# A softmax turned through DRAM: whole rows out and four strided loads back, against four strided stores and whole rows back

## The chip, the cores and the metric

The kernel runs on one core of one Trainium2 chip, in fp32. The metric is the device time of one execution in microseconds, taken as the median of several runs. A profiled execution is a run of its own; its span (first to last instruction of the program) is a little shorter than its device time.

## The reference, cut to what matters

The input is x of 8 batches, 256 positions, 256 features. Four residual blocks follow one another, each on a layer norm of x: attention A (16 heads of 128), a gated FFN that keeps the 32 largest of 512 logits, attention B (16 heads of 16, block causal mask, rotary embedding), and the same FFN again.

```
x = x + attn_a(layernorm(x))      # softmax(q k^T / sqrt(128)) v, then Wout
x = x + ffn(layernorm(x))         # top 32 of 512 logits, softmax, genes, tanh gate
x = x + attn_b(layernorm(x))      # masked softmax(q k^T / 4) v, then w_o
x = x + ffn(layernorm(x))
```

In both attentions TensorE needs the softmax with keys on the partitions, to multiply it with v; it is made with queries on the partitions. It has to be turned: each 256 x 256 matrix of A, each 128 x 128 piece of B. This turn is what the change is about.

## The kernel before

**Tiles and loops.** The program goes over the 8 batches; in each, 256 positions are two tiles of 128 partitions. `attn_a` (L492) makes per head q and k (`qk_proj`, matmuls L522, copied by ACT at L530), scores (`soft`, L543), the softmax (`softmax`: maximum L739 on DVE, exponential L745 on ACT, reciprocal L751 on DVE, the product L756 on GpSimd), per pair of heads the turn and the product with v (`attend` L551, matmuls L568, copied by ACT at L577), and per four heads the output projection (`project`, L589). `ffn` (L773) is a serial chain, mostly on DVE: L810 (MAX8) and L827 (match and replace) alternate four times; its matmuls are L784, L799, L841, L855, L869. `attn_b` (L905) works on four groups of 32 rows at a time: scores L1015, softmax (L1126, L1132, L1138, L1143), the turn of two groups at a time, and the product with v in `attend` (L1067, matmuls L1077).

**The turn.** `turn` (L442) takes two softmax tiles of 128 x 512. DVE's 32 x 32 block transpose (L450) turns each within its blocks and writes it to T [128, 2, 512], the blocks laid so that a row of T holds four chunks c, one for each group of 32 partitions that it must go to. What remains is to swap partition group g with chunk c. This goes through a DRAM tile D of 512 KB: one store of T (L454), and, when it has landed, four loads (L460), one for each c, into 32 partitions of PT, each picking 256 runs of 512 B. PT is then the moving operand of L568 or L1077. Each of the seven batches 0 to 6 has 8 such turns in A and 6 in B, 98 in all. The last batch turns on TensorE instead (L680, L1040) and has none.

**Buffers.** T has two buffers, PT six, D six. DVE may write T again once the store has landed; a load into PT waits for the matmuls that read the buffer last.

**What sets the order.** The order of every engine is worked out ahead by `Plan` (L53 to L206). Each operation is given to `do` with a cost: how long it holds its engine and how long until its result is there. `order` (L106) is a greedy list: the operation that can start first goes first, of those within 1 ns the one of the best priority. It follows buffers as well as data. For transfers, the queue SP is held for the first number; the second is time on one common data path (bytes / 330 GB/s, so 1.59 us for 512 KB and 0.40 for 128 KB), and the landing is 2.0 us after that (`FLIGHT`, L161 to L163). In the turn, each store and load has 450 ns for SP. The planned order is then kept: all loads and stores are issued by SP's one queue, in that order, and an instruction that waits there holds all behind it. Where TensorE has a planned gap of 0.8 us or more, `keep_warm` (L184) puts in transposes of the identity (profile line L1169).

The other transfers on that queue are the loads of x (L286, one of 128 KB for each tile, 128 runs of 1 KB) and the stores of the output (L1151, the same size).

Of the kernel before, what the change touches and what calls it, by code (L numbers as in the profile page):

```python
# [17 lines left out]
P = 128  # L18
TT = S // P
# [6 lines left out]
SQ = 32  # L26
# [183 lines left out]
def kernel(  # L210
# [19 lines left out]

    const = ctx.enter_context(tc.tile_pool(name="const", bufs=1))
    work = ctx.enter_context(tc.tile_pool(name="work", bufs=1))
    psum = ctx.enter_context(tc.tile_pool(name="psum", bufs=1, space=bass.MemoryType.PSUM))
    dram = ctx.enter_context(tc.tile_pool(name="dram", bufs=1, space=bass.MemoryType.DRAM))

    def sb(shape, tag, bufs):
        return plan.buf(work, shape, tag, bufs)
# [201 lines left out]
            pe, reads, [key],  # L439
        )  # L440

    def turn(sources, pT, views, pri, keys):  # L442

        T = sb([P, 2, 512], "T", 2)
        D = plan.buf(dram, [P, 2, 512], "D", 6)
        for j, (p, view) in enumerate(zip(sources, views)):
            do(
                "DVE", dve(512), lambda j=j, view=view: [nc.vector.transpose(*view(T()[:, j]))],  # L450
                pri, [(p, 0)], [(T, j)],
            )
        do(
            "SP", (450.0, 524288 / plan.RATE), lambda: [nc.sync.dma_start(D(), T())],  # L454
            pri, [(T, 0), (T, 1)], [(D, 0)],
        )
        for c in range(P // SQ):
            do(
                "SP", (450.0, 131072 / plan.RATE),
                lambda c=c: [nc.sync.dma_start(  # L460
                    pT()[ts(c, SQ)].rearrange("p h (g f) -> p h g f", f=P),
                    D().rearrange("(g i) h (c f) -> c i h g f", i=SQ, f=P)[c])],
                pri, [(D, 0)], [keys[c]],
            )


    def normed_a(b):
# [24 lines left out]
    def attn_a(b):  # L492
        xT, pe, ew = normed_a(b)
        vs, qks, ps_, ao = {}, {}, {}, {}

        def v_proj(g):
            for t in range(TT):
                v = sb([P, HG * DA], "Av", 4)
                pv = bank("A")
                for c in range(DC):  # L500
                    do(
                        "PE", mm(512),
                        lambda c=c, t=t, pv=pv: [nc.tensor.matmul(  # L503
                            pv(), xT()[:, c, ts(t, P)], wA[2, g][:, c, :],
                            start=c == 0, stop=c == DC - 1)],
                        pe(g * HG, 0.5), [(xT, 0), ("wA", 2, g)], [(pv, 0)], [v],
                    )
                do(
                    "ACT", act(512), lambda v=v, pv=pv: [nc.scalar.copy(v(), pv())],
                    ew(g * HG, 0.5), [(pv, 0)], [(v, 0)],  # L510
                )
                vs[g, t] = v

        def qk_proj(h):
            g, i = divmod(h, HG)
            pq = bank("A")
            qk = sb([P, 2, S], "Aqk", 4)
            for kind in range(2):
                for c in range(DC):
                    do(  # L520
                        "PE", mm(256),
                        lambda kind=kind, c=c: [nc.tensor.matmul(  # L522
                            pq()[:, ts(kind, S)], wA[kind, g][:, c, ts(i, DA)], xT()[:, c, :],
                            start=c == 0, stop=c == DC - 1)],
                        pe(h, 0), [(xT, 0), ("wA", kind, g)], [(pq, kind)], [qk],
                    )

            do(
                "ACT", act(512),
                lambda: [nc.scalar.activation(  # L530
                    qk().rearrange("p k s -> p (k s)"), pq(), AF.Copy, scale=float(DA ** -0.25))],
                ew(h, 0), [(pq, 0), (pq, 1)], [(qk, 0)],
            )
            qks[h] = qk

        def soft(h):
            qk = qks[h]
            sc = bank("A")
            p = scores_of("A")
            for t in range(TT):  # L540
                do(
                    "PE", mm(256),
                    lambda t=t: [nc.tensor.matmul(  # L543
                        sc()[:, ts(t, S)], qk()[:, 0, ts(t, P)], qk()[:, 1, :],
                        start=True, stop=True)],
                    pe(h, 1), [(qk, 0)], [(sc, t)], [p],
                )
            softmax(sc, [(sc, 0), (sc, 1)], p, TT, S, "A", ew(h, 1))
            ps_[h] = p

        def attend(h0):  # L551
            po = bank("A")
            a = sb([P, 2, S], "Aao", 3)
            pT = sb([P, 2, 512], "PT", 6)
            turn(
                [ps_[h0], ps_[h0 + 1]], pT,
                [lambda T, p=ps_[h0 + j]: (
                    T.rearrange("p (c k t q) -> p t k c q", c=4, k=TT, t=TT),
                    p().rearrange("p t (k c q) -> p t k c q", k=TT, c=4)) for j in range(2)],
                ew(h0 + 1, 2), [(pT, c) for c in range(4)],  # L560
            )
            for j in range(2):
                h = h0 + j
                g, i = h // HG, h % HG
                for k in range(TT):
                    do(
                        "PE", mm(256),
                        lambda j=j, k=k, g=g, i=i: [nc.tensor.matmul(  # L568
                            po()[:, ts(j, S)].rearrange("p (t g q) -> p t g q", t=TT, g=4),
                            vs[g, k]()[:, ts(i, DA)],  # L570
                            pT()[:, j].rearrange("p (g k t q) -> p k t g q", g=4, k=TT, t=TT)[:, k],
                            start=k == 0, stop=k == TT - 1)],
                        pe(h, 3), [*((pT, c) for c in range(4)), (vs[g, k], 0)], [(po, j)], [a],
                    )
            do(
                "ACT", act(512),
                lambda: [nc.scalar.copy(a().rearrange("p j q -> p (j q)"), po())],  # L577
                ew(h0 + 1, 3), [(po, 0), (po, 1)], [(a, 0)],
            )
            ao[h0] = a  # L580

        def project(g):
            hs = range(g * HG, (g + 1) * HG)
            py = bank("A")
            for t in range(TT):
                for h in hs:
                    do(
                        "PE", mm(256),
                        lambda t=t, h=h: [nc.tensor.matmul(  # L589
                            py()[:, ts(t, DIM)], ao[h - h % 2]()[:, h % 2, ts(t, P)],  # L590
                            woutT[:, h, :], start=h == hs[0], stop=h == hs[-1])],
                        pe(hs[-1], 4), [(ao[h - h % 2], 0), ("wout", g)], [(py, t)],
                    )
            for t in range(TT):
                x = xs[b, t]
                do(
                    "DVE", dve(256),
                    lambda t=t, x=x: [nc.vector.tensor_tensor(
                        x(), x(), py()[:, ts(t, DIM)], ALU.add)],
                    ew(hs[-1], 4), [(py, 0), (py, 1)], [(x, 0)],  # L600
                )

        for h in range(HA):
            if h % HG == 0:
                v_proj(h // HG)
            qk_proj(h)
            soft(h)
            if h % 2:
                attend(h - 1)
            if h % HG == HG - 1:  # L610
                project(h // HG)
# [293 lines left out]
    def attn_b(b, t):  # L905
# [94 lines left out]
        def scores(c, pT):  # L1000
# [50 lines left out]
            if b < B - 1:  # L1051
                for g in range(0, NR, 2):
                    turn(
                        ps_[g : g + 2], pT[g // 2],
                        [lambda T, p=p: (
                            T.rearrange("p (c i q) -> p i c q", c=4, i=4),
                            p().rearrange("p a (i c q) -> p (a i) c q", i=TT, c=4))
                         for p in ps_[g : g + 2]],
                        ew, [(pT[g // 2], ("c", c)) for c in range(4)],
                    )  # L1060

        def turned_p(pT, g, i):
            if b == B - 1:
                return pT[g // 2]()[:, g % 2, ts(i, P)]
            return pT[g // 2]()[:, g % 2].rearrange("p (g i q) -> p i g q", g=4, i=4)[:, i]

        def attend(c, pT):  # L1067

# [2 lines left out]
            def emit():  # L1071
                n = t + 1
                for par in range(2):
# [9 lines left out]

            do(
                "PE", (450.0 * (t + 1) + 150, 450.0 * (t + 1) + 150 + plan.DRAIN), emit, pe(5),
                [*((pair, k) for pair in pT for k in (0, 1, *(("c", c) for c in range(4)))),
                 *((vbs[b, k], par) for k in range(t + 1) for par in range(2))],
                [(po, 0)], [ctxt],
            )
# [136 lines left out]
```

## Time and profile before

| | us |
|---|---|
| median of 3 runs | 1022.26 (1022.11 to 1028.04) |
| the profiled execution, device time | 1023.49 |
| its span | 1021.7 |
| matmuls of L1169 (identity), busy | 28.7, of it 26.8 after 894 us |
| POOL, ACT busy | 380.6, 468.8 |
| DMA queue of SP: 133936 packets, 117.71 MB | 36.3% of 16 engines' span |
| SP waiting for a store of T to land (L460) | 155.0, 67 times |
| SP waiting for a transpose on DVE (L454) | 199.0, 42 times |
| the chain that ended last: PE, DVE, DMA, SP's queue | 55%, 16%, 14%, 7% |

A row of a group or a line gives engine, operation, written tile <- read tiles, count, and durations. PE is TensorE's matmuls, DVE VectorE, ACT ScalarE, POOL GpSimd, SP the queue engine. "A <- B: 11.7, 11, 1.8" in the waits means that A's engine stood idle before A until B was done, 11.7 us in total, in 11 places, 1.8 us at the longest. A wait for several things is put down to the last. Engines are pipelined, so a busy matmul of 380 ns follows another one after 214 ns; only the last one of a run shows its full length.

### The profile page before, as it was taken

The numbers are of one execution on the slowest core, as the hardware profiler recorded it, in microseconds if no ns is written. First come the engines' busy times: TensorE is split into PE (matmuls) and PEld (weight loads), VectorE is DVE, ScalarE is ACT, GpSimd is POOL, SyncE is SP. The second block draws the span as 40 slices with busy tenths as digits, with TensorE's granted clock in tenths as the row PEclk, the third lists the DMA queues.
The fourth block names the chain that finished last, engine by engine and source line by source line (L and its number), as shares of the span: only waits on it lengthen the run. The fifth ranks groups of instructions, "written<-read, shape, count | busy, mean of one in ns | idle before, by whom it ended". The sixth has DMA issues, their size and how long they took to land.

```text
span 1021.7 us, 16959 instructions
## 1 busy us (share of the span) xinstructions
PE 971.1 (95%) x5843; PEld 730.8 (72%) x5843; DVE 681.7 (67%) x1670; ACT 468.8 (46%) x1503; POOL 380.6 (37%) x484
## 2 busy tenths in 40 slices
PE   7999999999999999999999999999999999999786
PEld 6777677676777777676776777667777668786664
DVE  2523867657676876759666686865867686688755
ACT  3433455443654445534644445634455335542261
POOL 2502245231553345323643335423354225542150
PEclk9999999999999999999999999999999999999988
DMA  9723225622266224642266223633136400420000
GB/s 331 253 95 104 83 81 183 191 78 68 93 216 187 78 68 145 189 131 93 83 185 187 82 84 129 203 113 119 56 134 201 126 6 21 136 93 11 1 2 11
DMA packets 134021, 118.78 MB, mean 116 GB/s; under 512 B 10160, under 2 KB 117808, under 8 KB 133936
## 3 DMA queue, kind: packets, MB, share of 16 engines
q1 hardware_dynamic: 133936, 117.71, 36.3%
q8 instruction: 46, 0.75, 0.3%
q14 instruction: 39, 0.32, 0.1%
HBM read 64.20 MB, written 53.48 MB: 115 GB/s over the span
## 4 chain that ended last, share of the span: by engine, by line
PE 55%; DVE 16%; DMA 14%; SPq 7%; issue 3%; POOL 3%; ACT 2%; POOLq 0%; DVEq 0%; ACTq 0%
PE ps L522 10%; PE ps L568 6%; DMA D<-T 6%; DMA PT<-D 6%; PE ps L589 6%; SPq L460 5%; PE ps L543 5%; PE ps L503 5%; DVE Fleft L827 4%; DVE Fm L810 4%; PE ps L799 3%; PE ps L869 2%; PE ps L1077 2%; PE ps L937 2%; PE ps L643 2%
## 5 line engine op out<-in xcount | busy, mean ns | idle before, releaser
L756 POOL TENSOR_TENSOR p<-p,Asm 128x512 f32<-128x512 f32 x128 | 135.0, 1056 | 303.3 <-DVE Asm L751 298.8
L522 PE MATMUL ps<-AxT,wqk 128*128 128x256 f32 x896 | 220.9, 381 | 0.0
L522 PEld LDWEIGHTS ps<-AxT,wqk 128*128 128x128 f32 x896 | 168.2, 191 | 26.2 <-issue 4.7
L450 DVE STREAM_TRANSPOSE T<-p 128x512 f32<-128x512 f32 x196 | 136.0, 702 | 57.3 <-POOL p L756 38.1
L745 ACT ACTIVATE p<-ps,Anm 128x256 f32<-128x256 f32 x256 | 119.1, 474 | 83.9 <-DVE Anm L739 80.0
L1143 POOL TENSOR_TENSOR p<-p,Bsm 128x512 f32<-128x512 f32 x96 | 99.0, 1042 | 102.8 <-DVE Bsm L1138 102.5
L739 DVE TENSOR_REDUCE Anm<-ps 128x2 f32<-128x512 f32 x128 | 87.3, 683 | 61.7 <-PE ps L543 58.7
L568 PE MATMUL ps<-PT,Av 128*128 128x256 f32 x448 | 110.3, 385 | 15.4 <-DMA PT<-D 12.0
L1132 ACT ACTIVATE p<-ps,Bnm 128x128 f32<-128x128 f32 (+1 forms) x256 | 106.2, 438 | 39.9 <-DVE Bnm L1126 29.6
L543 PE MATMUL ps<-Aqk 128*128 128x256 f32 x448 | 120.4, 382 | 0.0
L568 PEld LDWEIGHTS ps<-PT,Av 128*128 128x128 f32 x448 | 81.9, 190 | 46.0 <-issue 25.4
L589 PE MATMUL ps<-woutT,Aao 128*128 128x256 f32 x448 | 112.9, 385 | 0.1
L530 ACT ACTIVATE Aqk<-ps 128x512 f32<-128x512 f32 x112 | 67.3, 601 | 97.7 <-PE ps L522 97.3
L503 PE MATMUL ps<-wv,AxT 128*128 128x512 f32 x224 | 106.5, 594 | 0.0
L543 PEld LDWEIGHTS ps<-Aqk 128*128 128x128 f32 x448 | 82.9, 190 | 24.8 <-issue 14.6
L589 PEld LDWEIGHTS ps<-woutT,Aao 128*128 128x128 f32 x448 | 82.1, 190 | 21.4 <-issue 7.7
L1126 DVE TENSOR_REDUCE Bnm<-ps 128x2 f32<-128x512 f32 (+1 forms) x96 | 66.3, 690 | 3.0
L810 DVE MAX8 Fm<-Fleft 128x8 f32<-128x512 f32 x96 | 66.2, 690 | 2.3
L577 ACT COPY Aao<-ps 128x512 f32<-128x512 f32 x56 | 32.9, 587 | 70.8 <-PE ps L568 70.8
L827 DVE MATCH_REPLACE8 Fleft<-Fm,Fleft 128x512 f32<-128x512 f32 x96 | 64.9, 676 | 0.0
L799 PE MATMUL ps<-wcT,FxT 128*128 128x512 f32 x128 | 61.5, 598 | 0.8 <-ACT FxT L790 0.8
L503 PEld LDWEIGHTS ps<-wv,AxT 128*128 128x128 f32 x224 | 41.5, 190 | 28.3 <-issue 25.0
(118 smaller groups left out, 1380.6 us busy)
## 6 DMA issues: line engine op xcount, KB each, us to landing
D<-T SPq DMA_DIRECT2D x98, 512.0 KB, 3.0
PT<-D SPq DMA_DIRECT2D x392, 128.0 KB, 3.2
wqk<-in_wqkvT_dram SPq DMA_DIRECT2D x8, 512.0 KB, 9.2
x<-in_x_dram SPq DMA_DIRECT2D x16, 128.0 KB, 2.3
wv<-in_wqkvT_dram SPq DMA_DIRECT2D x4, 512.0 KB, 9.7
woutT<-in_woutT_dram SPq DMA_DIRECT2D x4, 512.0 KB, 10.3
out_dram<-x SPq DMA_DIRECT2D x16, 128.0 KB, 1.7
wcT<-in_wcT_dram SPq DMA_DIRECT2D x1, 512.0 KB, 9.5
```

Source lines behind the costliest of these rows:

```text
L450: "DVE", dve(512), lambda j=j, view=view: [nc.vector.transpose(*view(T()[:, j]))],
L503: lambda c=c, t=t, pv=pv: [nc.tensor.matmul(pv(), xT()[:, c, ts(t, P)], wA[2, g][:, c, :], start=c == 0, stop=c == DC - 1)],
L522: lambda kind=kind, c=c: [nc.tensor.matmul(pq()[:, ts(kind, S)], wA[kind, g][:, c, ts(i, DA)], xT()[:, c, :], start=c == 0, stop=c == DC - ...
L543: lambda t=t: [nc.tensor.matmul(sc()[:, ts(t, S)], qk()[:, 0, ts(t, P)], qk()[:, 1, :], start=True, stop=True)],
L568: lambda j=j, k=k, g=g, i=i: [nc.tensor.matmul(po()[:, ts(j, S)].rearrange("p (t g q) -> p t g q", t=TT, g=4), vs[g, k]()[:, ts(i, DA)], p ...
L589: lambda t=t, h=h: [nc.tensor.matmul(py()[:, ts(t, DIM)], ao[h - h % 2]()[:, h % 2, ts(t, P)], woutT[:, h, :], start=h == hs[0], stop=h == ...
L745: lambda i=i: [nc.scalar.activation(p()[:, i, :], s3()[:, i, :], AF.Exp, bias=nm()[:, i : i + 1], accum_out=sm()[:, i : i + 1])],
L756: lambda: [nc.gpsimd.tensor_tensor(p(), p(), sm().unsqueeze(2).to_broadcast((P, n, k)), ALU.mult)],
L810: lambda r=r, src=src: [nc.vector.max(m8[r](), src())],
L827: lambda r=r, src=src: [nc.vector.match_replace(left(), m8[r](), src(), TAKEN)],
L1132: lambda i=i: [nc.scalar.activation(p3()[:, i, :], s3()[:, i, :], AF.Exp, bias=nm()[:, i : i + 1], accum_out=sm()[:, i : i + 1])],
L1143: lambda: [nc.gpsimd.tensor_tensor(p3(), p3(), sm().unsqueeze(2).to_broadcast((P, n, k)), ALU.mult)],
```

## The change

In `turn` the two sides of the round trip change places. T is laid out as [128, 4, 256]: chunk c is the outer step, and within it the two heads (or groups) lie beside each other, so that a run for one destination is 256 elements (1 KB) rather than two of 128. Four stores, one for each partition group g of 32, write the runs of T to D where they belong: row (c, i), column group g. One load of 128 rows of 4 KB then brings D back to PT as it is. D's layout becomes the final one of PT, (g, h, f), and the matmuls of both attentions read PT by it: their moving operand steps 256 instead of 128 elements from one partition group's piece to the next. The planner's numbers follow: 360 ns of SP for each of the five transfers in place of 450, the bytes moved to the other side (128 KB for a store, 512 KB for the load); the load depends on all four stores, each store on both transposes, and PT has two keys, both written by the one load, in place of four. The line that opens the DRAM pool moves up by one.

```diff
--- before.py
+++ after.py
@@ -230,8 +230,8 @@
 
     const = ctx.enter_context(tc.tile_pool(name="const", bufs=1))
     work = ctx.enter_context(tc.tile_pool(name="work", bufs=1))
+    dram = ctx.enter_context(tc.tile_pool(name="dram", bufs=1, space=bass.MemoryType.DRAM))
     psum = ctx.enter_context(tc.tile_pool(name="psum", bufs=1, space=bass.MemoryType.PSUM))
-    dram = ctx.enter_context(tc.tile_pool(name="dram", bufs=1, space=bass.MemoryType.DRAM))
 
     def sb(shape, tag, bufs):
         return plan.buf(work, shape, tag, bufs)
@@ -439,29 +439,32 @@
             pe, reads, [key],
         )
 
-    def turn(sources, pT, views, pri, keys):
-
-
-
-        T = sb([P, 2, 512], "T", 2)
-        D = plan.buf(dram, [P, 2, 512], "D", 6)
+    def turn(sources, pT, views, pri):
+
+
+
+        T = sb([P, 4, 256], "T", 2)
+        D = plan.buf(dram, [P, 4, 256], "D", 6)
         for j, (p, view) in enumerate(zip(sources, views)):
             do(
-                "DVE", dve(512), lambda j=j, view=view: [nc.vector.transpose(*view(T()[:, j]))],
+                "DVE", dve(512),
+                lambda j=j, view=view: [nc.vector.transpose(
+                    *view(T().rearrange("p c (h f) -> p h c f", h=2)[:, j]))],
                 pri, [(p, 0)], [(T, j)],
             )
-        do(
-            "SP", (450.0, 524288 / plan.RATE), lambda: [nc.sync.dma_start(D(), T())],
-            pri, [(T, 0), (T, 1)], [(D, 0)],
-        )
-        for c in range(P // SQ):
-            do(
-                "SP", (450.0, 131072 / plan.RATE),
-                lambda c=c: [nc.sync.dma_start(
-                    pT()[ts(c, SQ)].rearrange("p h (g f) -> p h g f", f=P),
-                    D().rearrange("(g i) h (c f) -> c i h g f", i=SQ, f=P)[c])],
-                pri, [(D, 0)], [keys[c]],
-            )
+        for g in range(4):
+            do(
+                "SP", (360.0, 131072 / plan.RATE),
+                lambda g=g: [nc.sync.dma_start(
+                    D().rearrange("(c i) g f -> g i c f", i=SQ)[g], T()[ts(g, SQ)])],
+                pri, [(T, 0), (T, 1)], [(D, g)],
+            )
+        do(
+            "SP", (360.0, 524288 / plan.RATE),
+            lambda: [nc.sync.dma_start(
+                pT().rearrange("p h f -> p (h f)"), D().rearrange("p g f -> p (g f)"))],
+            pri, [(D, g) for g in range(4)], [(pT, 0), (pT, 1)],
+        )
 
 
     def normed_a(b):
@@ -555,9 +558,9 @@
             turn(
                 [ps_[h0], ps_[h0 + 1]], pT,
                 [lambda T, p=ps_[h0 + j]: (
-                    T.rearrange("p (c k t q) -> p t k c q", c=4, k=TT, t=TT),
+                    T.rearrange("p c (k t q) -> p t k c q", k=TT, t=TT),
                     p().rearrange("p t (k c q) -> p t k c q", k=TT, c=4)) for j in range(2)],
-                ew(h0 + 1, 2), [(pT, c) for c in range(4)],
+                ew(h0 + 1, 2),
             )
             for j in range(2):
                 h = h0 + j
@@ -568,9 +571,10 @@
                         lambda j=j, k=k, g=g, i=i: [nc.tensor.matmul(
                             po()[:, ts(j, S)].rearrange("p (t g q) -> p t g q", t=TT, g=4),
                             vs[g, k]()[:, ts(i, DA)],
-                            pT()[:, j].rearrange("p (g k t q) -> p k t g q", g=4, k=TT, t=TT)[:, k],
+                            pT().rearrange("p h f -> p (h f)").rearrange(
+                                "p (g h k t q) -> p h k t g q", g=4, h=2, k=TT, t=TT)[:, j, k],
                             start=k == 0, stop=k == TT - 1)],
-                        pe(h, 3), [*((pT, c) for c in range(4)), (vs[g, k], 0)], [(po, j)], [a],
+                        pe(h, 3), [(pT, 0), (pT, 1), (vs[g, k], 0)], [(po, j)], [a],
                     )
             do(
                 "ACT", act(512),
@@ -1053,16 +1057,17 @@
                     turn(
                         ps_[g : g + 2], pT[g // 2],
                         [lambda T, p=p: (
-                            T.rearrange("p (c i q) -> p i c q", c=4, i=4),
+                            T.rearrange("p c (i q) -> p i c q", i=4),
                             p().rearrange("p a (i c q) -> p (a i) c q", i=TT, c=4))
                          for p in ps_[g : g + 2]],
-                        ew, [(pT[g // 2], ("c", c)) for c in range(4)],
+                        ew,
                     )
 
         def turned_p(pT, g, i):
             if b == B - 1:
                 return pT[g // 2]()[:, g % 2, ts(i, P)]
-            return pT[g // 2]()[:, g % 2].rearrange("p (g i q) -> p i g q", g=4, i=4)[:, i]
+            return pT[g // 2]().rearrange("p h f -> p (h f)").rearrange(
+                "p (g h i q) -> p h i g q", g=4, h=2, i=4)[:, g % 2, i]
 
         def attend(c, pT):
 
@@ -1083,7 +1088,7 @@
 
             do(
                 "PE", (450.0 * (t + 1) + 150, 450.0 * (t + 1) + 150 + plan.DRAIN), emit, pe(5),
-                [*((pair, k) for pair in pT for k in (0, 1, *(("c", c) for c in range(4)))),
+                [*((pair, k) for pair in pT for k in range(2)),
                  *((vbs[b, k], par) for k in range(t + 1) for par in range(2))],
                 [(po, 0)], [ctxt],
             )
```

## The prediction

> **What bounds the kernel now.** I first read the page's busy shares, then TensorE's waits in the stretch where turns run (51 to 894 us), then one turn on the chain of waits, then the transfers one by one.
>
> The first row of the page:
>
> ```profile
> PE 971.1 (95%) x5843; PEld 730.8 (72%) x5843; DVE 681.7 (67%) x1670; ACT 468.8 (46%) x1503; POOL 380.6 (37%) x484
> ```
>
> TensorE sets the pace; no other engine is near full. What can be won is TensorE's idle time: in 51 to 894 us the table of windows has PE busy 818.5 of 843.0 us, so 24.5 us idle. The waits of PE in that window (us in total, times, longest):
>
> ```profile
> PE ps L568 <- DMA PT<-D: 11.7, 11, 1.8
> PE ps L1077 <- DMA PT<-D: 6.2, 7, 1.6
> PE ps L855 <- ACT FwT L847: 2.3, 5, 0.6
> ```
>
> 17.9 of the 24.5 us end with the landing of a turned softmax, in 18 waits of 1.0 us on average, none over 1.8. Outside it, another 0.5 us waits for PT. So the turn bounds nothing in most places, but it is late by about a microsecond in every fifth of the 98 turns. The ends are different: 894 to 1021.7 us hold no turn for TensorE beyond the first few us, and there its idle time (20.6 us by the windows) belongs to DVE, ACT and POOL.
>
> One such turn on the chain of waits (start, us, what):
>
> ```profile
> 116.89 0.62 DVE T L450
> 117.51 0.02 issue
> 117.53 4.76 DMA D<-T
> ...
> 122.34 0.56 SPq L460
> 122.90 0.05 issue
> 122.95 0.61 SPq L460
> 123.56 0.05 issue
> 123.61 0.60 SPq L460
> 124.21 0.04 issue
> 124.26 3.09 DMA PT<-D
> 127.34 0.04 issue
> 127.39 1.99 PE ps L568 x8
> ```
>
> From the transpose's end to the first matmul 9.9 us go by in three pieces: the store's landing, SP issuing three more loads behind the first (1.92 us), and the last load's landing. Over all 98 turns, the last transpose's end to the last landing takes 9.65 us in the mean and 7.5 at least: 0.81 until SP gets to the store, 3.19 for the store, 0.36 until the first load is issued, 5.30 for the four loads.
>
> **The change, part by part.** What each transfer costs, from the rows of the two lines (count, min/median/max ns to issue; then us to landing), and the page's part 6:
>
> ```profile
> L454 SPq DMA_DIRECT2D D<-T x98: 319/326/1219, 35.4 to 905.9; - x98
> DMA to landing us min/median/max: 2.6/3.0/5.0
> ```
> ```profile
> L460 SPq DMA_DIRECT2D PT<-D x392: 557/607/1702, 39.5 to 910.5; - x196
> DMA to landing us min/median/max: 2.7/3.2/4.7
> ```
> ```profile
> x<-in_x_dram SPq DMA_DIRECT2D x16, 128.0 KB, 2.3
> out_dram<-x SPq DMA_DIRECT2D x16, 128.0 KB, 1.7
> ```
>
> (1) Issue. 128 runs of 4 KB cost SP 0.326 us, 256 runs of 512 B cost 0.607. A new store has 32 rows x 4 runs = 128 runs: at least 0.326, at most 0.607; I take 0.35, since x and the output, also 128 runs, take 0.34. With 0.03 between issues, four stores take 4 x 0.35 = 1.4 us and the load 0.33. Per turn 1.8 us of SP instead of 0.33 + 4 x 0.64 = 2.9; over 98 turns 176 instead of 284 us.
>
> (2) Data. In windows holding one kind of packet alone, busy share x 16 engines / packets gives 29 ns for 512 B (92.0 to 98.5 us), 47 ns for 1 KB (an output store, 204.7 to 206.5) and 160 ns for 4 KB (109.3 to 112.0). Per turn and engine: before 8 x 160 + 64 x 29 = 3.1 us, after 32 x 47 + 8 x 160 = 2.8. A small gain.
>
> (3) The store stage. An output store of the same size and run length lands in 1.7 us undisturbed. The fourth new store is issued at 3 x 0.35 = 1.05 and lands at 2.75 if alone; the engines need 4 x 0.38 = 1.5 us for all four, about the rate of the issue, so I take 2.9. Before: 2.6 undisturbed. This part of the change costs 0.3 us. The store's rows are read from 32 partitions and written 4 KB apart; no row of the trace stores so, the nearest being the four loads (32 partitions, 512 B runs), whose packets fit the same line through the sizes. Bounds: 2.6 and, if each packet took twice its time, 4.4.
>
> (4) The load stage. An x load lands in 1.97 us undisturbed, 8 packets of 1 KB per engine (0.4 us) within it. With 8 of 4 KB (1.3 us): 1.97 - 0.4 + 1.3 = 2.9 us. Bounds: 2.6 (what the equally large store takes) and 3.6. Before: 4.8 to 5.0 undisturbed, 1.9 of them SP's issue of the later three.
>
> Sum, undisturbed: before 2.6 + 0.05 + 5.0 = 7.7 us, after 2.9 + 0.06 + 2.9 = 5.9: 1.8 us less. In the mean, with the same disturbance on each piece (x 1.2 on stores, x 1.1 on the load) and a shorter wait for SP (0.5): 0.5 + 3.5 + 0.3 + 3.3 = 7.6 instead of 9.65: 2.0 us less.
>
> [...] Were the four stores to run wholly one behind another, the stage would be 4 x 1.7 = 6.8 us and the turn 9.8, worse than 7.7. The trace's own four partition slices do not behave so: issued 0.64 apart, each lands about 3.1 us after its issue, all four in 5.0 and not 4 x 2.7 = 10.8. They share engines but overlap their fixed part. I go by the row. [...] Here the same 128 KB take 1.7 us to DRAM and 2.0 from it, so I keep 2.9.
>
> (5) Waits. The load waits for four stores instead of one: three more semaphores, at 17 to 28 ns each by SP's rows, under 0.1 us. Behind it in SP's queue stand other turns' stores, x loads and output stores; "L460 <- DMA D<-T" holds SP for 155 us now. The hold behind the last issue shrinks from 2.3 to about 1.5 us per turn, so all of them gain. T (two buffers) is freed 0.3 us later; DVE waits for it six times, 10.4 us in all, so 2 us more on an engine with a third of its time free. TensorE waits on one semaphore in place of four per turn: nothing, PE's semaphore instructions (51 ns) run under earlier matmuls. The transposes and matmuls keep their numbers and sizes; only steps change from 128 to 256 elements, with runs of 32 as before: nothing, and were each of the 196 transposes 10% slower (0.07 us) DVE would still cover 14 us.
>
> (6) The plan's numbers. In the planner's own arithmetic a turn is 7.4 us before (1.59 + 2.0, then four loads 0.45 apart) and 7.25 after. So it leaves about the same work between a softmax and its use; but any change of a due time reorders the list, and the order of all engines comes out anew. Nothing in the trace prices that. I bound it by TensorE's idle time in this stretch that is no turn's, 24.5 - 17.9 = 6.6 us: it could be 6 us less or twice that, 13 us, more; I take 0.
>
> **Sum.** With the order unchanged, TensorE does the same work between a softmax and its use, so a wait shrinks by what the turn got faster. All 18 waits are at most 1.8 us and the turn gains 1.8 to 2.0: some 18 us close, and 20 x 0.165 us of refilling the array, counted as busy, with them: 21. What is given back: TensorE comes sooner to L855 and the other points of the FFN, which DVE's serial chain sets; I take a third, 7 us. 1023.5 (the profiled execution: span 1021.7 and 1.8 around it) - 14 = 1009.5. The median shown is 1.2 lower: **1008 us**.
>
> **Rivals.** (a) The gain is handed back: TensorE's waits on DMA close, and waits on ACT, DVE or POOL or a worse order take most of it. For: every order around the FFN hangs on DVE, 67% busy in long chains. Against: only 6.6 us of waits are others' now. 1022 - 5 = 1017, between 1012 and 1030. (b) The stores are ordered: if the program's tracking of DRAM takes the four interleaved slices of D as overlapping, each store waits for the one before. Place: SP, between the stores. Stage 3 x 1.75 + 1.75 = 7.0, turn 9.9 undisturbed, 2.2 us more than now, and SP held 5.3 us more per turn. The 18 waits grow by 2.2 (40 us), and with SP held some 30 others start at about 0.5: 1022 + 55 = 1077. It decides as soon as one store's landing lies between two issues. Against: the loads, slices of PT, are issued 0.64 apart; but they are slices in SBUF, and no interleaved DRAM write is in this trace. (c) The new order is plainly worse, or the store stage is near its upper bound 4.4: 1022 + 13 = 1035. (d) No hand-back, and the order gains: 1022 - 21 - 5 = 996.
>
> **How the numbers follow.** Forecast 0.48 (its own range 1000 to 1012), (d) 0.05, (a) 0.29, (c) 0.10, (b) 0.08. About 1% is what a measurement tells from no change: faster 0.53, same 0.29, slower 0.18. The range leaves out (b) and the far sides of (c) and (d): 996 to 1040.
>
> **What would show it.** Right: issues of 0.35 us, stores landed 2.9 and the load 2.9 us after the first issue undisturbed, PE's waits for PT under 5 us, L460 and L454's SP time near 176 us. Wrong: semaphore waits of 1.7 us between stores (b); PE's waits for PT gone but as much idle before L855, L841, L784 (a); a store stage over 4 us, or PE idle outside the turns' waits above 13 us (c).

## The result, and the profile after

| | before | changed |
|---|---|---|
| median of 6 runs, us | 1024.14 (1022.11 to 1028.04) | 1013.64 (1011.17 to 1016.69) |
| ratio | | 0.9894, 95% interval 0.9866 to 0.9922 |
| span of the profiled execution, us | 1021.7 | 1012.9 |
| last transpose's end to the last landing in PT: mean (least), us | 9.65 (7.5) | 9.31 (6.9) |
| the stores' stage: mean (least), us | 3.19 (2.6) | 4.70 (3.6) |
| the loads' stage: mean (least), us | 5.30 (4.8) | 3.88 (3.1) |
| SP issuing the turns' transfers, us in all | 280 | 211 |

The stores' stage runs from the first store's issue to the last store's landing, the loads' stage likewise; "least" is the shortest of the 98 turns, and below it is called undisturbed.

Forecast was 1008 us, 14 us less; measured are 10.5 us less. But the turn, which was to become 2.0 us shorter in the mean, became 0.34 us shorter. So the size came out nearly right although one step was wrong by far, and the question of the experiments is how 98 turns that are scarcely shorter can save 10 us.

The page of the changed kernel, TensorE's row and the transfers of SP's queue (share of 16 engines):

```profile
PE 968.6 (96%) x5834; PEld 730.7 (72%) x5834; DVE 674.9 (67%) x1670; ACT 467.5 (46%) x1503; POOL 378.5 (37%) x484
...
q1 hardware_dynamic: 83760, 117.71, 39.9%
```

TensorE still sets the pace. There are 50,176 packets fewer, as counted ahead, yet the engines' share rose from 36.3% where it should have fallen. TensorE's waits in 51 to 894 us:

```profile
PE ps L571 <- DMA PT<-D: 9.3, 12, 1.3
PE ps L1082 <- DMA PT<-D: 5.1, 9, 1.5
PE ps L788 <- DVE Fxn L428: 1.2, 2, 0.6
PE ps L859 <- ACT FwT L851: 0.8, 1, 0.8
```

Waits for PT went from 17.9 to 14.4 us, not to under 5, and none is over 1.5. TensorE's other idle time in this stretch did not grow: 843.0 - 825.4 - 14.4 = 3.2 us, where it was 6.6 (L855, now L859, had 2.3 us of waits). The rows of the stores' line and of the load's line:

```profile
L458 SPq DMA_DIRECT2D D<-T x392: 302/438/2190, 35.5 to 894.7; - x196
...
DMA to landing us min/median/max: 2.0/2.7/5.6
```
```profile
L464 SPq DMA_DIRECT2D PT<-D x98: 337/338/363, 40.0 to 899.1; - x98
...
DMA to landing us min/median/max: 3.1/3.6/5.5
```

A first store takes SP 0.30 us, one right behind another 0.44, and none lands in less than 2.0 us. The two buffers of T come free later with the stores: DVE's waits for them, 10.4 us in 6 places before, are now

```profile
DVE T L451 <- DMA D<-T: 26.1, 18, 4.0
```

SP, too, now waits 169.5 us at the loads for stores to land, 155.0 before.

One stretch of the chain of waits, and after it SP's own timeline of another (start, us, what):

```profile
424.64 0.02 SPq L458
424.65 0.04 issue
424.70 0.38 SPq L458
425.07 0.04 issue
425.12 0.45 SPq L458
425.56 0.04 issue
425.61 0.44 SPq L458
426.05 0.04 issue
426.09 0.52 SPq L458
...
426.78 4.63 DMA PT<-D
431.41 0.04 issue
431.46 1.56 PE ps L571 x6
```
```profile
545.95 0.45 SPq L458 DMA_DIRECT2D D<-T  x1
546.57 0.34 SPq L464 DMA_DIRECT2D PT<-D  x1
547.27 1.29 SPq L458 DMA_DIRECT2D D<-T  x3
548.73 0.35 SPq L464 DMA_DIRECT2D PT<-D  x1
549.13 0.49 SPq L458 DMA_DIRECT2D D<-T  x1
```

The part before the load, one issue of SP after another, has become long. And the new plan, for which each store is an operation of its own, puts another turn's load between the stores of a turn. In 13 of the 98 turns the four stores do not stand together; their stage takes 7.0 us in the mean, that of the other 85 takes 4.35.

### The profile page after: what moved, and what is told of

Its sections match the earlier page's. It is cut to its first block, busy times and chain, and to the rows that moved or that the text cites. A ratio compares the mean times of both kernels' runs of the same rounds, so it can differ in the third digit from the quotient of the medians.

```text
span 1012.9 us, 16898 instructions
## 1 busy us (share of the span) xinstructions
PE 968.6 (96%) x5834; PEld 730.7 (72%) x5834; DVE 674.9 (67%) x1670; ACT 467.5 (46%) x1503; POOL 378.5 (37%) x484
## 4 chain that ended last, share of the span: by engine, by line
PE 63%; DMA 14%; DVE 14%; SPq 3%; POOL 2%; issue 2%; ACT 1%; DVEq 0%; POOLq 0%; ACTq 0%
PE ps L525 13%; DMA D<-T 7%; PE ps L593 7%; DMA PT<-D 7%; PE ps L571 7%; PE ps L546 7%; PE ps L506 6%; PE ps L803 3%; DVE Fleft L831 3%; SPq L458 3%; DVE Fm L814 3%; DVE T L451 3%; PE ps L873 2%; PE ps L941 2%; PE ps L647 2%
## 5 line engine op out<-in xcount | busy, mean ns | idle before, releaser
L1137 ACT ACTIVATE p<-ps,Bnm 128x128 f32<-128x128 f32 (+1 forms) x256 | 106.0, 440 | 36.3 <-DVE Bnm L1131 30.4
L546 PEld LDWEIGHTS ps<-Aqk 128*128 128x128 f32 x448 | 83.7, 190 | 23.2 <-issue 10.4
L890 POOL TENSOR_TENSOR Fup<-Fup,Fdown 128x256 f32<-128x256 f32 x30 | 22.2, 740 | 102.7 <-DVE Fup L884 56.1
## 6 DMA issues: line engine op xcount, KB each, us to landing
woutT<-in_woutT_dram SPq DMA_DIRECT2D x4, 512.0 KB, 10.4
```

The lines of the kernel that those rows point to most:

```text
L546: lambda t=t: [nc.tensor.matmul(sc()[:, ts(t, S)], qk()[:, 0, ts(t, P)], qk()[:, 1, :], start=True, stop=True)],
L1137: lambda i=i: [nc.scalar.activation(p3()[:, i, :], s3()[:, i, :], AF.Exp, bias=nm()[:, i : i + 1], accum_out=sm()[:, i : i + 1])],
```

## The experiments

Theory M: the moves themselves save the time, by the turn's length in the places where TensorE waits for it. Theory O: the plan's numbers changed the order of all engines, and the new order saves the time. The two can be parted, since the plan only decides the order: an operation of the plan may issue other transfers than it was planned for. The kernel before had medians of 1027.3, 1027.1 and 1021.9 us beside the experiments (1024.1 beside the change), so each run is judged by its ratio to the kernel before that was timed beside it, with the 95% interval in brackets. Spans are those of the profiled executions; "waits for PT" is TensorE's idle time until a turn landed, over the whole span (before 18.4, changed 15.2).

### Order of before, moves of the change; and the reverse

e1_order_before: the kernel before, with the layouts of the change; its one store operation issues the four stores, its first load operation the one load, the other three issue nothing.

```diff
-lambda: [nc.sync.dma_start(D(), T())],
+lambda: (nc.sync.dma_start(
+    D().rearrange("(c i) g f -> g i c f", i=SQ)[g], T()[ts(g, SQ)]) for g in range(4)),
...
-lambda c=c: [nc.sync.dma_start(...)],      # 256 runs of 512 B
+lambda c=c: [] if c else [nc.sync.dma_start(
+    pT().rearrange("p h f -> p (h f)"), D().rearrange("p g f -> p (g f)"))],
```

> The transfers of the change, with every instruction of TensorE, DVE, ACT and GpSimd in the order of the kernel before. Theory M (the moves: a shorter turn and a freer SP queue close TensorE's waits): nearly the whole gain, 1012 to 1016 us, TensorE's waits for PT in 51 to 894 us at 14 us or less. Theory O (the order that the new plan came out with, not the moves: the turn is only 0.3 us shorter in the mean): 1020 to 1026 us, waits for PT near 17 us.

e2_order_after is the mirror image: the plan of the change, whose first store operation issues the one store and whose load operation issues the four loads.

> The mirror image: the order of the changed kernel on the four compute engines, with the one store and four loads of before. Theory M: the gain is gone, 1021 to 1027 us, waits for PT at 18 us or more. Theory O: the gain stays, 1011 to 1016 us.

| | span | ratio to before (95%) | waits for PT | turn, mean |
|---|---|---|---|---|
| e1: order before, moves changed | 1006.9 | 0.9817 (0.9788 to 0.9846) | 11.1 | 9.15 |
| e2: order changed, moves before | 1020.7 | 0.9976 (0.9949 to 1.0003) | 24.5 | 9.84 |

In both, every instruction of TensorE, DVE, ACT and GpSimd stands in the same place as in the kernel whose order it has (in e1's trace the starts of eight of 5,843 matmuls are exchanged with a neighbour's, within 0.1 us). Theory M holds and O falls: the moves alone save 1.8%, more than the whole change and more than M's own range, and the order alone saves nothing that is sure. TensorE's waits for PT in e1:

```profile
PE ps L571 <- DMA PT<-D: 8.8, 8, 2.3
...
PE ps L1082 <- DMA PT<-D: 2.3, 4, 0.8
```

Since the order is the same, each turn of e1 can be set against the same turn of before. 31 turns of before kept TensorE waiting for more than 0.05 us just ahead of a matmul on PT. They were the long ones, 11.0 us in the mean against 9.0 for the other 67. In e1 these 31 take 10.0, the other 67 take 8.75. The parts of the 31, before and then: until SP gets to the store 1.49 and 1.15, the stores 3.61 and 4.69, until the load is issued 0.53 and 0.22, the loads 5.38 and 3.96. So the turn lost a microsecond just where it counted, and only a quarter where it didn't; a mean over all turns hides that. The 31 were picked by one execution of before, so a part of their larger gain may come from the picking. TensorE's idle time just ahead of matmuls on PT goes from 22.2 to 12.6 us.

### The plan's numbers alone

e3_after_450 is the changed kernel with 450 in place of 360 ns, e4_before_360 the kernel before with 360 in place of 450.

```diff
-"SP", (360.0, 131072 / plan.RATE)        # e3; and the load's 360.0 likewise
+"SP", (450.0, 131072 / plan.RATE)
```

> The changed kernel with 450 ns of SP for each of the five transfers, as before; only the order comes out anew. Theory M: 1010 to 1017 us, as the moves are the same. Theory O: a new draw of the order, so anywhere from 1005 to 1026 us, and most likely not the same as the changed kernel's 1013.6.

> The kernel before with 360 ns for each of its five transfers in the plan; the moves stay as they were, only the order comes out anew. Theory M: 1021 to 1028 us (the plan is further from the 607 ns that a load really takes, so if anything slower). Theory O: a new draw of the order, anywhere from 1010 to 1030 us.

e3: 0.9852 (0.9820 to 0.9885), span 1008.6, waits for PT 18.6 us, as many as before; across different orders these waits alone do not tell the time, since the other waits change with the order too. e4: 0.9970 (0.9954 to 0.9986), span 1019.8. Both lie within the ranges of either theory and so do not part them. With the moves of before, the three orders (before, e2, e4) lie within 0.3%, far less than the moves bring. With the moves of the change, three orders give 0.9817, 0.9852 and 0.9894; the number of turns whose stores are parted by another transfer is 0, 8 and 13 in them. That fits, but no run changed the parting alone.

### Which of the moves

e5_loads_1KB keeps the one whole store and the order of before. T has the layout of the change, so that each of the four loads takes 128 runs of 1 KB.

```diff
-pT()[ts(c, SQ)].rearrange("p h (g f) -> p h g f", f=P),
-D().rearrange("(g i) h (c f) -> c i h g f", i=SQ, f=P)[c])],
+pT()[ts(c, SQ)].rearrange("p h (g f) -> p (h g) f", f=256),
+D().rearrange("(g i) c f -> c i g f", i=SQ)[c])],
```

> Order of before. One whole store as before, T laid out as in the change, so that each of the four loads picks 128 runs of 1 KB instead of 256 of 512 B: the run length alone, without moving the strided side. If the gain is the length of the runs (issue 0.48 apart instead of 0.64, half the packets): load stage 4.3 us instead of 5.0, turn 0.7 us shorter, two thirds of the gain, 1011 to 1016 us. If it is the one load at the end (nothing issued behind the first load): little, 1018 to 1025 us.

0.9803 (0.9771 to 0.9834), span 1001.2: as much as e1, with the strided side left where it was. Both expectations are missed on the low side; the one by the length of the runs is the nearer. Issue of the four loads takes SP 1.73 us undisturbed instead of 2.52, the loads' stage 4.3 instead of 4.8, the turn 8.92 us in the mean. TensorE's waits for PT in e5:

```profile
PE ps L570 <- DMA PT<-D: 3.1, 7, 1.2
...
PE ps L1081 <- DMA PT<-D: 1.0, 1, 1.0
```

e8_load_in_four is e1 with the one load cut into four of 32 whole rows.

```diff
-lambda c=c: [] if c else [nc.sync.dma_start(
-    pT().rearrange("p h f -> p (h f)"), D().rearrange("p g f -> p (g f)"))],
+lambda c=c: [nc.sync.dma_start(
+    pT()[ts(c, SQ)].rearrange("p h f -> p (h f)"),
+    D()[ts(c, SQ)].rearrange("p g f -> p (g f)"))],
```

> As e1_order_before, with the one load cut into four of 32 whole rows, issued one after another. If the merged load is where the gain comes from: load stage 4.2 us instead of 3.2 undisturbed, SP 1 us more per turn, and half the gain or more is lost, 1014 to 1022 us. If the gain is elsewhere (strided side, run length): 1007 to 1011 us.

1.0040 (1.0019 to 1.0061), span 1028.0, waits for PT 22.2 us, turn 9.92 us: the whole gain is lost and a little more, which is beyond the range expected. With four stores, the one load carries all of it. Four loads of 32 runs take SP 1.69 us (0.42 each when close behind another), no less than four of 128 runs.

e7_store_in_four is the kernel before with only its store cut into four of 32 whole rows.

```diff
-lambda: [nc.sync.dma_start(D(), T())],
+lambda: (nc.sync.dma_start(D()[ts(g, SQ)], T()[ts(g, SQ)]) for g in range(4)),
```

> Order and loads of before; only its one store is cut into four of 32 whole rows (32 runs of 4 KB each). If slices of 32 partitions are what makes stores slow: packets of 4 KB at 200 ns and more, store stage 3.2 us or more instead of 2.6. If it is the scattering in 1 KB runs: packets stay at 160 ns and the stage at 2.6 to 2.9. Time: 0.3 to 1 us more per turn and 0.9 us more of SP, so 1026 to 1036 us by the theory that the turn's length sets TensorE's waits; 1024 to 1028 if it does not.

1.0532 (1.0487 to 1.0578), span 1080.4, turn 11.07 us:

```profile
PE ps L569 <- DMA PT<-D: 36.0, 30, 2.5
PE ps L1078 <- DMA PT<-D: 18.3, 16, 2.1
```

The price is higher than either theory said: a turn 1.4 us longer adds 35.9 us of waits for PT and 58.7 us of span. A part of the span may be the clock: the mean granted clock of TensorE was 0.983 over the six runs of e7 and 0.994 over those of the kernel before beside them; if busy time goes as the clock, 1.1% of 971 us is some 11 us (an estimate). The cutting alone brings the stores' stage from 2.6 to 3.44 us undisturbed, and the packets of 4 KB, all of them in the trace, from 167 to 231 ns. The scattering in 1 KB runs adds 0.2 to that (3.64 in e1).

### Why sliced stores are slow

The DMA's rate (40 equal parts of a window): before, one store of 128 partitions alone (109.3 to 112.0 us), then e1, the four stores of one turn alone (131.0 to 134.9 us):

```profile
GB/s 0 0 0 0 0 0 0 0 0 0 0 0 0 425 425 425 364 303 485 425 485 364 485 303 303 485 425 485 364 364 485 303 61 0 0 0 0 0 0 0
```
```profile
GB/s 0 0 0 0 0 0 0 0 0 137 221 200 231 168 168 189 190 210 189 210 147 158 189 231 357 378 389 316 284 242 189 200 126 63 0 0 0 0 0 0
```

The first two slices of 32 partitions move at some 190 GB/s, a store of all 128 at 400; only in the middle, where the second and third slice meet, does the rate rise, to 389. That cutting into slices is the cause is shown by e7, where nothing is scattered. Why a slice is slow is not shown by it. e6 asks whether it matters which slice follows which.

e6_g0213 is e1 with the stores in the order 0, 2, 1, 3.

> As e1_order_before, with the four stores issued in the order g = 0, 2, 1, 3. [...]

0.9833 (0.9799 to 0.9867), span 1007.0; all packets of 1 KB 57.4 ns in the mean against 59.5 in e1, stage 3.56 us undisturbed instead of 3.64. In time it hardly helps. But the rate of one undisturbed turn (133.4 to 137.2 us, again four slices of 128 KB) now rises twice, in the second and in the fourth slice:

```profile
GB/s 0 0 0 0 0 0 0 0 86 194 183 183 183 183 173 205 335 367 313 162 205 248 237 259 259 151 140 183 302 377 356 205 33 0 0 0 0 0 0 0
```

So the order does set which slices are fast: in e1 the peak of 389 GB/s lies where the second and third meet, in e6 the second slice reaches 367 and the fourth 377. It does not make the stage short: the first slice, which follows none, stays at some 185, the third gets no more than 259, and the stage gains 0.08 us. What holds the slices back is not shown.

e9_two_queues is e1 with the stores 1 and 3 issued by ACT.

```diff
-lambda: (nc.sync.dma_start(
+lambda: ((nc.scalar if g % 2 else nc.sync).dma_start(
```

> As e1_order_before, with stores 1 and 3 of each turn issued from ACT's queue. If the turn's length is what sets TensorE's waits: store stage about 3.0 us instead of 3.65 undisturbed, turn 0.6 us or more shorter, waits for PT under 6 us, 1000 to 1006 us. If ACT (which now waits for DVE's transposes in its own order and issues 196 stores of some 0.45 us, 88 us more on an engine busy for 468) becomes what others wait for: 1010 to 1030 us.

0.9914 (0.9895 to 0.9933), span 1014.0. The issue of four stores takes 0.85 us instead of 1.75, but their stage still 3.71 us undisturbed: it is not SP's issue that makes it long. TensorE's waits for PT fall to 3.3 us all the same (11.1 in e1), and half of the gain is lost elsewhere:

```profile
PE ps L546 <- ACT Aqk L533: 3.8, 2, 2.8
PE ps L941 <- ACT BxT L929: 3.6, 4, 1.6
PE ps L571 <- DMA PT<-D: 2.7, 5, 1.1
```

ACT has become what TensorE waits for: 15.8 us in all, 4.9 in e1. In this run the turns' waits are gone and the gain is handed back, as rival (a) had it for the change.

### The held queue or the turn's own length

e10_idle_loads is e1 with three loads of 4 bytes, which nobody reads, issued on SP behind each turn's load. This is extra work.

```diff
-lambda c=c: [] if c else [nc.sync.dma_start(
+lambda c=c: [nc.sync.dma_start(idle[0:1, next(turns) % 64 :][:, 0:1], scale_d)] if c else [
+    nc.sync.dma_start(
```

> As e1_order_before, with three idle loads of 4 bytes issued on SP behind each turn's load (extra work; the results do not use it). SP is held some 1.0 us more per turn, as in e8_load_in_four, but a turn that finds SP free is not longer. If SP's held time is what counts: most of the gain is lost, as in e8, 1018 to 1030 us. If the turn's own length counts: only those turns that stand behind another in the queue are later, 1008 to 1014 us.

0.9855 (0.9836 to 0.9874), span 1007.7, waits for PT 7.7 us. SP issues 77 us more in all, 0.8 us per turn; the ratio is 0.4% above that of e1, with intervals that overlap. From the transpose's end to the load's issue 5.33 us go by instead of 5.22. SP's held time by itself counts for little; e8, with 1.3 us more per turn but in the turn's own path, lost everything.

### A faster version

e11_e5_order_after has the moves of e5 and the compute engines in the order of the change. e12_e5_measured is e5 with the plan's numbers at the measured 340 ns (store) and 480 ns (loads).

> The moves of e5_loads_1KB with the compute engines in the order of the changed kernel. If that order costs some 0.7% whatever moves are as short as the change's: 1012 to 1017 us. If the order costs only with the change's own moves: 1005 to 1009 us.

> e5_loads_1KB with the plan's numbers at what was measured, 340 ns for the store and 480 for each load; the order comes out anew. If new orders scatter without direction: 1003 to 1015 us. If orders planned with truer numbers fit the moves better: 1000 to 1006 us.

e11: 0.9767 (0.9750 to 0.9783), median 998.4. e12: 0.9756 (0.9740 to 0.9771), median 997.4, span 995.5. Both beat before and the change, and both lie below all that was expected of them. For e11, that order does not cost 0.7% with other moves; it saves a little against e5 (0.9803). What costs with the moves of the change is therefore not the compute engines' order by itself, and the parted stores, which e11 cannot have, stay the best guess. TensorE's waits for PT in e12:

```profile
PE ps L570 <- DMA PT<-D: 2.2, 4, 0.8
PE ps L1081 <- DMA PT<-D: 1.7, 3, 0.8
```

## Why the prediction was right, and where it was wrong

Right in direction and near in size. That the size came so near is in part luck: the turn gained far less than was summed up, the turns that count gained more than the mean, and the loss that came with the plan happened to be about as large as the one put down to the FFN. By its own steps:

**What bounds the kernel: right.** With one order and different moves, TensorE's waits for PT and the span go together: e5 4.1 and 1001.2 us, e1 11.1 and 1006.9, before 18.4 and 1021.7, e8 22.2 and 1028.0, e7 54.3 and 1080.4. Two runs with this order do not fit the row: e10 (7.7 and 1007.7) slightly, and e9 (3.3 and 1014.0), where ACT takes over.

**(1) Issue: too low.** 0.35 was taken for each store, from x and output transfers. Those rows are mostly single transfers; behind another, an issue takes 0.44 and the next follows after 0.48. SP's sum is 211, not 176 us. The trace of before had this: its first load of four took 557, the following 607 ns.

**(2) and (3), the failed step: the stores' stage.** 2.9 us undisturbed was predicted, 3.64 measured, and 4.70 in the mean instead of 3.5. The working took 47 ns for a packet from the output store, which reads 128 partitions, and took it that stores of slices overlap because four loads into slices overlapped well. In the window of four undisturbed stores that was read for this (103.7 to 107.6 us of the changed kernel), 53.9% busy of 16 engines x 3.9 us over 512 packets is 66 ns. The loads did overlap, but spaced 0.64 us apart they needed only 128 KB per 0.64 us, 205 GB/s, close to what a stored slice got (some 190 in e1). They were no evidence for stores that come 0.48 apart. The stores do not run wholly one behind another (that would be 6.8 us), but in e1 the first two slices together got some 190 GB/s, where a store of 128 partitions in the trace of before got 400.

**(4) The load: nearly right.** 2.9 predicted, 3.1 to 3.2 undisturbed, 3.88 in the mean. Its packets of 4 KB were priced at the 160 ns of a store's; in a window with one load alone (107.6 to 110.9 us of the changed kernel, 46.7% of 16 engines over 128 packets) they took 193, and 8 x 33 ns are 0.26 us, about what was missing.

**(5) The buffers and the queue: wrong.** DVE's waits for T were to grow by 2 us and grew by 15.7; SP's waits for stores to land were to shrink and grew from 155.0 to 169.5. Both fit the longer stores' stage. What they cost in time is not shown; in e5, with the one store, DVE waits 6.8 us.

**Sum of the turn: wrong.** 5.9 undisturbed and 7.6 in the mean were predicted; 6.9 and 9.3 came. The gain was to be 2.0 us and was 0.34.

**The gain from the waits: right for another reason.** 18 us of waits and 3 of refilling were to close, since every turn would be faster by as much as the longest wait. With the order kept (e1), 14.8 us of span went, and 15.2 between TensorE's first and last matmul: 8.8 of idle time and 6.4 of busy time. But not all turns got faster by as much; those that kept TensorE waiting did by 1.0 us. Of the 6.4, 2.4 is put down to refilling ahead of matmuls on PT (what lies between two starts above the usual step, less the idle time), and the mean granted clock, 0.992 and then 0.994, would make about 2 (0.2% of 965 us); both are estimates, and the other 2 us are not assigned.

**What is given back: right in size, wrong in place.** A third, 7 us, was to go to the FFN's waits. Those did not grow (L855: 2.3, then 0.8). What was given back is the difference between e1 and the change, 6 us in span and some 8 by the ratios 0.9817 and 0.9894, and it came with the plan: (6) had been taken as nothing. That the parting of the four stores on SP does it is argued from the counts of e1, e3 and the change and from e11. A kernel with the order of the change and its four stores kept together would settle it and was not tried.

**Rivals.** (b) did not occur: the four stores were issued 0.48 apart, with none waiting for another's landing. (c)'s slow store stage did occur in the mean, but the load's gain was larger.

## What to carry to other kernels

Take a transfer's packet time and issue time from a row that is like it in partitions and in spacing, or leave the bounds wide: here the 47 ns of a 1 KB packet from 128 partitions were 66 ns in stores of 32, and the 0.34 us of a single issue 0.44 behind another. Where an engine waits in a fifth of the places, work out the change for those places; the mean over all can be off by several times. When a change replaces one planned transfer by several, look at what the planner puts between them. And before moving the strided side of a round trip, try longer runs on the side where it is: here that alone brought 2.0%, and 2.3 and 2.4% in two other orders (e11, e12). That the measured numbers in e12's plan are what helped is not shown, as e11, planned with others, is as fast.

## What the runs showed of the hardware that was not expected

SP's issue took nearly the same for 32 and for 128 runs: 32 runs of 4 KB (e7, e8) and 128 of 1 KB (the change, e5) both took 0.42 to 0.44 us when close behind another transfer and 0.30 as the first of four; 256 runs of 512 B (before) took 0.61 and 0.56.

The first of four stores of 32 partitions moved at some 190 GB/s (e1, e6), a store of 128 partitions at 400 (before). In the four of one turn of e1 the rate rose to 389 GB/s where the second and third slice met; in one of e6, with the order 0, 2, 1, 3, it rose to 367 in the second slice and 377 in the fourth. Issuing slices 1 and 3 from a second queue (e9) gained nothing in the time until all had landed (3.71 against 3.64 us). Another pairing of the slices on two queues was not tried.
